# Cross-attention on one core: loads in slices and in order of use, two sets of transposes moved to the front, the mask arithmetic on another engine, the last group's normalisation in two parts

## The chip, the cores and the metric

The kernel runs on one core of one Trainium2 chip. The metric is device time in microseconds (us) of one execution; lower is better. The core has five engines that run side by side: TensorE (PE in the profile; PEld is its weight load), VectorE (DVE), ScalarE (ACT), GpSimd (POOL) and SyncE (SP). Each takes its own instructions strictly in order and waits for others by semaphores. Loads and stores are issued here from SP and ACT, each through a queue of its own, and are carried out by 16 DMA engines that both queues share.

## The reference

Cross-attention with 8 heads of width 256, 16 batches, 256 queries and 77 keys in each batch, all in float32, then a residual and a layer normalisation:

```python
Q = (img_embed @ Wq).reshape(B, -1, H, D).transpose(0, 2, 1, 3)     # img_embed = x (16, 256, 256)
K = (sent_embed @ Wk).reshape(B, -1, H, D).transpose(0, 2, 1, 3)    # sent_embed = context (16, 77, 192)
V = (sent_embed @ Wv).reshape(B, -1, H, D).transpose(0, 2, 1, 3)
score = jnp.einsum('bhqd,bhkd->bhqk', Q, K) / math.sqrt(D)
score = jnp.where((atten_mask != 0)[:, None, None, :], score, -jnp.inf)
attn = jax.nn.softmax(score, axis=-1)
ctx = jnp.einsum('bhqk,bhkd->bqhd', attn, V).reshape(B, -1, H * D)
out = ctx @ Wo + img_embed
mu = jnp.mean(out, axis=-1, keepdims=True)
var = jnp.var(out, axis=-1, keepdims=True)
return (out - mu) * jax.lax.rsqrt(var + EPS) * gamma + beta
```

## The kernel before

Neither Q, K nor V is formed. Per head two products of weights are made once: G = Wq Wk^T / sqrt(D), kept transposed in `gT`, and U = Wv Wo, in `u`. Then, per batch, A = G c^T (`a`, four batches at a time) and VW = c U (`vw`), and for each tile of 128 queries the scores x A (`ps`), a softmax over 77 keys for each of 8 heads (`s`, `e`, `p`), the transposes of `p` (`pp`, copied to `pT`), the sum over heads of p VW (`po`), the residual and the statistics for the normalisation (`mv`).

The program has three stages.

1. **Once.** All loads are issued at the head of the program: on SP's queue Wq in two halves, Wv, the first group of x (`xg`, 8 tiles of 128 rows, 1 MB), the mask `m_i`, gamma, beta and the second group of x; on ACT's queue Wk in two halves, the context `c_sb` and Wo. For each head TensorE then transposes the rows of Wq and Wk (`p_wqT`, `p_wkT`, by `transposed`) and multiplies them (`pg`); then it transposes the context in 22 pieces (`pc`, copied to `cT`), and for each head transposes Wv (`p_wvT`) and multiplies by Wo (`pu`). Transposes land in PSUM; `evacuate` copies them to SBUF, in turn by ACT and DVE. So the copies of `p_wqT` fall to ACT and those of `p_wkT` to DVE. Five small DVE operations turn the mask into `bias` and `live`.
2. **The batches.** Four groups of four batches, 8 query tiles each. `prepare_group` transposes the group's x (`px`, copied to `xT`) and makes `a` (64 matmuls `pa`); then tiles follow, with the attention of a tile two tiles behind its scores.
3. **The end of a group.** When the last tile of a group is done, one square root and one reciprocal over its 8 tiles, then 8 operations that scale and shift (line 313), and a store for each two tiles.

The order on each engine is that of the program as a scheduler rearranges it: it may move an independent instruction ahead of others on its engine, and once built the order is fixed. Buffers are pooled: the weights and the mask live in the pool `wload`, whose memory is given back after stage 1 and is taken over by `a` and other tiles of stage 2, so the first copy into `a` waits for the last readers of that pool. Loads and stores share eight completion semaphores in rotation: the ninth is issued when the first has landed, and so on.

Of the kernel before, what the change touches and what calls it, by code (L numbers as in the profile page):

```python
# [27 lines left out]
# so neither Q, K, V nor the context of a head is ever formed.  # L28
@with_exitstack
def kernel(  # L30
# [25 lines left out]

# [38 lines left out]

# [1 line left out]
    with tc.tile_pool(name="wload", bufs=1) as wp, tc.tile_pool(name="wt", bufs=2) as wt:  # L97
# [8 lines left out]
        wv_r = wv.rearrange("(t p) f -> p t f", p=LP)  # L106
        half = H * D // 2
        for i in range(2):
            cols = slice(i * half, (i + 1) * half)
            nc.sync.dma_start(wq_sb[:, :, cols], wq_r[:, :, cols])  # L110
            nc.scalar.dma_start(wk_sb[:, :, cols], wk_r[:, :, cols])
        nc.scalar.dma_start(c_sb, c_rows)
        nc.sync.dma_start(wv_sb, wv_r)
        nc.scalar.dma_start(wo_sb, wo.rearrange("(t p) f -> p t f", p=P))
        load_x(0)
        nc.sync.dma_start(m_i, mask.rearrange("b k -> (b k)").partition_broadcast(P))
        nc.sync.dma_start(gam, gamma.partition_broadcast(P))
        nc.sync.dma_start(bet, beta.partition_broadcast(P))
        load_x(1)

        def transposed(w_sb, rows, h, tag):
# [12 lines left out]
            return t_sb  # L134

        for h in range(H):
            wqT = transposed(wq_sb, P, h, "wqT")
            wkT = transposed(wk_sb, LP, h, "wkT")
            pg = ps_mm.tile([P, 2, DI], F32, tag="mm", name=f"pg_{h}")
            for lc in range(2):  # L140
                for dc in range(2):
                    nc.tensor.matmul(  # L142
                        pg[:LP, lc, :],
                        wkT[:, dc, lc * LP : (lc + 1) * LP],
                        wqT[:, dc, :],
                        start=(dc == 0),
                        stop=(dc == 1),
                    )
            nc.scalar.mul(gT[:, :, h, :], pg[:LP], D ** -0.5)

        for r in range(0, NCR, 2):
# [9 lines left out]
            for lc in range(2):  # L161
# [3 lines left out]
                )  # L165

        for h in range(H):
            wvT = transposed(wv_sb, LP, h, "wvT")
            pu = ps_mm.tile([P, 2, DI], F32, tag="mm", name=f"pu_{h}")
            for lc in range(2):  # L170
                for dc in range(2):
                    nc.tensor.matmul(  # L172
                        pu[:LP, lc, :],
                        wvT[:, dc, lc * LP : (lc + 1) * LP],
                        wo_sb[:, 2 * h + dc, :],
                        start=(dc == 0),
                        stop=(dc == 1),
                    )
# [13 lines left out]
    ap = ctx.enter_context(tc.tile_pool(name="ap", bufs=2))  # L192
    sp = ctx.enter_context(tc.tile_pool(name="sp", bufs=3))
    st = ctx.enter_context(tc.tile_pool(name="st", bufs=4))

    xT_of, a_of, vw_of, p_of, mv_of = {}, {}, {}, {}, {}

    def prepare_group(g):
        xg = xg_of[g]
        xT = xp.tile([P, 2, GT * P], F32, tag="xT", name=f"xT_{g}")  # L200
        for j in range(0, GT, 2):
            pt = ps_tr.tile([P, 4, P], F32, tag="tr", name=f"px_{g}_{j}")
            for dc in range(2):
                for i in range(2):
                    nc.tensor.transpose(  # L205
                        pt[:, 2 * dc + i, :], xg[:, j + i, dc * P : (dc + 1) * P], ident
                    )
            evacuate(
                xT[:, :, j * P : (j + 2) * P],
                pt.rearrange("p (dc i) m -> p dc (i m)", dc=2),  # L210
            )
        xT_of[g] = xT
        a = ap.tile([P, 2, GB, H, S2], F32, tag="a", name=f"a_{g}")
# [87 lines left out]

    def normalise_group(g):
        mv, yg = mv_of[g], xg_of[g]
        std = st.tile([P, GT], F32, tag="std", name=f"std_{g}", bufs=2)
        nc.scalar.activation(std, mv[:, :, 1], AF.Sqrt, bias=eps)
        rstd = st.tile([P, GT], F32, tag="rstd", name=f"rstd_{g}", bufs=2)
        nc.vector.reciprocal(rstd, std)
        for j in range(GT):
            y = yg[:, j, :]
# [13 lines left out]
    for t in range(NT + AHEAD):  # L323
# [44 lines left out]
```

## Time and profile before

| | us |
|---|---|
| median of 3 runs (lowest, highest) | 482.4 (482.24, 482.61) |
| the profiled execution, first to last instruction (span) | 480.1 |
| TensorE busy in the span | 439.0 (91%) |
| VectorE busy | 210.7 (44%) |
| ScalarE busy | 136.8 (28%) |
| GpSimd busy | 39.6 (8%) |

The profile covers one execution, from its first instruction to its last; of this execution no other time is on record than its span. The median of the runs is 2.3 us above the span. A busy share is an average over the three stages; a view by stretches shows each for itself.

### The profile page before, as it was taken

What the parts mean: (1) busy time and instruction counts of PE and PEld (TensorE: products, weight loads), DVE (VectorE), ACT (ScalarE), POOL (GpSimd) and SP (SyncE); (2) the same over time, 40 slices, a digit from 0 to 9 for tenths busy, and PEclk for the clock granted to TensorE, in tenths of its full rate; (3) what the DMA queues carried; (4) which work ended last, traced back from release to release, by engine and by line L of the source; (5) the groups of instructions that cost most, each with busy time, mean ns of one, the idle gap of its engine ahead of it and who ended that gap; (6) DMA issues with size and microseconds to landing.
All of it is one profiled execution on the core that took longest, in us unless ns stands there. A gap on an engine that the chain in (4) does not pass through costs nothing.

```text
span 480.1 us, 4689 instructions
## 1 busy us (share of the span) xinstructions
PE 439.0 (91%) x1846; PEld 298.3 (62%) x1846; DVE 210.7 (44%) x424; ACT 136.8 (28%) x242; POOL 39.6 (8%) x38
## 2 busy tenths in 40 slices
PE   1409899999999999999999999999999999999993
PEld 1307677755765875758567766585767756658572
DVE  0031223235736433375373433844735238555364
ACT  1103422223132222251333213523132134331321
POOL 0000000012112000121111101112111011121110
PEclk9859999999999999999999999999999999999997
DMA  8993000000000000022000000130000000200002
GB/s 237 256 341 106 0 1 1 0 2 0 0 1 0 1 0 0 1 87 89 0 0 1 0 0 2 53 123 0 1 1 0 1 0 1 89 0 0 2 1 87
DMA packets 13446, 17.86 MB, mean 37 GB/s; under 512 B 480, under 2 KB 12208, under 8 KB 13232
## 3 DMA queue, kind: packets, MB, share of 16 engines
q1 hardware_dynamic: 9696, 12.95, 8.9%
q10 hardware_dynamic: 3728, 4.62, 3.3%
q8 instruction: 14, 0.23, 0.2%
q14 instruction: 8, 0.07, 0.0%
HBM read 13.37 MB, written 4.19 MB: 37 GB/s over the span
## 4 chain that ended last, share of the span: by engine, by line
PE 87%; DMA 6%; DVE 3%; ACT 2%; issue 0%; DVEq 0%; ACTq 0%
PE po L293 24%; PE pv L234 22%; PE pa L218 14%; PE ps L250 14%; PE pp L289 5%; DMA m_i<-in_mask_BxS_if_dram 5%; PE pg L142 3%; PE pu L172 3%; DMA wk_sb<-in_L_xattn_Wk_dram 2%; PE px L205 2%; DVE wkT L94 1%; ACT pT L290 1%; DVE xg L313 1%; PE p_wkT L126 0%; PE p_wvT L126 0%
## 5 line engine op out<-in xcount | busy, mean ns | idle before, releaser
L293 PE MATMUL po<-vw,pT 77*128 77x256 f32 x512 | 117.2, 382 | 1.7 <-ACT pT L290 1.7
L234 PE MATMUL pv<-u,cT 96*77 96x512 f32 x256 | 113.1, 593 | 0.1
L293 PEld LDWEIGHTS po<-vw,pT 77*128 77x128 f32 x512 | 94.6, 190 | 21.3 <-ACT pT L290 9.7
L234 PEld LDWEIGHTS pv<-u,cT 96*77 96x77 f32 x256 | 37.5, 148 | 67.0 <-issue 57.8
L250 PE MATMUL ps<-a,xT 128*128 128x308 f32 x256 | 75.8, 422 | 0.0
L277 POOL TENSOR_TENSOR p<-e,rden 128x616 f32<-128x616 f32 x32 | 38.9, 1216 | 423.1 <-DVE rden L275 236.5
L218 PE MATMUL pa<-cT,gT 96*128 96x308 f32 x256 | 67.7, 422 | 0.0
L241 ACT COPY vw<-pv 77x512 f32<-77x512 f32 x64 | 37.1, 581 | 97.8 <-PE pv L234 97.5
L297 DVE TENSOR_TENSOR xg<-po,xg 128x256 f32<-128x256 f32 x32 | 13.6, 424 | 108.8 <-PE po L293 108.7
L290 ACT COPY pT<-pp 77x512 f32<-77x512 f32 x64 | 34.1, 583 | 86.5 <-PE pp L289 86.5
L218 PEld LDWEIGHTS pa<-cT,gT 96*128 96x128 f32 x256 | 48.0, 190 | 16.6
L250 PEld LDWEIGHTS ps<-a,xT 128*128 128x128 f32 x256 | 46.5, 190 | 12.4 <-issue 0.5
L289 PEld LDWEIGHTS pp<-ident,p 128*77 128x77 f32 x256 | 30.4, 148 | 11.3 <-issue 5.3
L94 DVE COPY a<-pa 128x308 f32<-128x308 f32 x32 | 15.3, 479 | 48.1 <-PE pa L218 48.1
L272 DVE TENSOR_REDUCE den<-e 128x8 f32<-128x616 f32 x32 | 25.4, 794 | 23.5 <-ACT e L270 23.4
L142 PE MATMUL pg<-wqT,wkT 128*96 128x256 f32 x64 | 18.9, 447 | 18.2 <-DVE wkT L94 18.2
L289 PE MATMUL pp<-ident,p 128*77 128x128 f32 x256 | 33.2, 272 | 0.0
L258 DVE TENSOR_TENSOR s<-ps,bias 128x616 f32<-128x616 f32 x32 | 25.6, 799 | 10.7 <-PE ps L250 10.7
L270 ACT ACTIVATE e<-s 128x616 f32<-128x616 f32 x32 | 22.9, 717 | 23.5 <-DVE s L266 23.4
L92 ACT COPY a<-pa 128x308 f32<-128x308 f32 x32 | 13.4, 418 | 48.3 <-PE pa L218 48.3
L142 PEld LDWEIGHTS pg<-wqT,wkT 128*96 128x96 f32 x64 | 11.6, 192 | 23.5 <-DVE wkT L94 19.8
L266 DVE TENSOR_TENSOR s<-s,top 128x616 f32<-128x616 f32 x32 | 25.6, 800 | 1.0
(45 smaller groups left out, 212.8 us busy)
## 6 DMA issues: line engine op xcount, KB each, us to landing
xg<-in_x_dram SPq DMA_DIRECT2D x4, 1024.0 KB, 12.5
out_dram<-xg SPq DMA_DIRECT2D x16, 256.0 KB, 2.2
wq_sb<-in_L_xattn_Wq_dram SPq DMA_DIRECT2D x2, 1024.0 KB, 12.3
wo_sb<-in_L_xattn_Wo_dram ACTq DMA_DIRECT2D x1, 2048.0 KB, 39.0
wk_sb<-in_L_xattn_Wk_dram ACTq DMA_DIRECT2D x2, 768.0 KB, 11.3
wv_sb<-in_L_xattn_Wv_dram SPq DMA_DIRECT2D x1, 1536.0 KB, 22.1
c_sb<-in_ctx_dram ACTq DMA_DIRECT2D x1, 924.0 KB, 27.3
m_i<-in_mask_BxS_if_dram SPq DMA_DIRECT2D x1, 616.0 KB, 21.7
```

What stands on the lines that cost most here:

```text
L142: nc.tensor.matmul(pg[:LP, lc, :], wkT[:, dc, lc * LP : (lc + 1) * LP], wqT[:, dc, :], start=(dc == 0), stop=(dc == 1),)
L218: nc.tensor.matmul(pa.rearrange("p b k -> p (b k)"), gT[:, lc, h, dc * P : (dc + 1) * P], cT[:, lc, g * GB * S2 : (g + 1) * GB * S2], star ...
L234: nc.tensor.matmul(pv[:S2], cT[:, lc, b * S2 : (b + 1) * S2], u[:, lc, 2 * n : 2 * n + 2, :].rearrange("p h d -> p (h d)"), start=(lc == 0 ...
L241: nc.scalar.copy(vw[:, 2 * n : 2 * n + 2, :].rearrange("p h d -> p (h d)"), pv[:S2])
L250: nc.tensor.matmul(ps[:, hh, :HK], xT_of[g][:, dc, j * P : (j + 1) * P], a_of[g][:, dc, bl, hh * 4 : hh * 4 + 4, :].rearrange("p h k -> p ...
L258: nc.vector.tensor_tensor(s.rearrange("p (a h) k -> p a h k", a=2), ps[:, :, :HK].rearrange("p a (h k) -> p a h k", k=S2), bias[:, b, :].u ...
L266: nc.vector.tensor_tensor(s, s, top.unsqueeze(2).to_broadcast([P, H, S2]), ALU.subtract)
L272: nc.vector.tensor_reduce(den, e, AX.X, ALU.add)
L277: nc.gpsimd.tensor_tensor(p, e, rden.unsqueeze(2).to_broadcast([P, H, S2]), ALU.mult)
L289: nc.tensor.transpose(pt[:S2, i, :], p[:, hh * 4 + i, :], ident)
L290: nc.scalar.copy(pT[:, hh * 4 : hh * 4 + 4, :], pt[:S2])
L293: nc.tensor.matmul(po, pT[:, h, :], vw_of[b][:, h, :], start=(h == 0), stop=(h == H - 1))
```

## The change

Four things are changed.

- **Loads.** The context goes first, its two parts on both queues; all else is issued by SP in order of use: the first group of x, then Wq and Wk in four slices of two heads each, Wv and Wo in two halves each, the second group of x, the mask, gamma, beta. The number of loads rises from 12 to 19. ACT issues one.
- **Transposes.** The transposes of the context and of the first group of x are ahead of the weight products on TensorE, and their copies ahead of the weights' copies on ACT and DVE.
- **Mask.** `bias` and `live` are computed by 14 GpSimd instructions (a compare, nine multiplications that fold 77 columns to one, four small or final ones); DVE has none of them.
- **Last group.** For the last of the four groups, the first six tiles are normalised and stored after the sixth; the last two after the eighth. The other groups are as before.

```diff
+        mid = NCR // 2
+        nc.scalar.dma_start(c_sb[:, :mid, :], c_rows[:, :mid, :])
+        nc.sync.dma_start(c_sb[:, mid:, :], c_rows[:, mid:, :])
+        load_x(0)
+        for h in range(0, H, 2):
+            cols = slice(h * D, (h + 2) * D)
             nc.sync.dma_start(wq_sb[:, :, cols], wq_r[:, :, cols])
-            nc.scalar.dma_start(wk_sb[:, :, cols], wk_r[:, :, cols])
-        nc.scalar.dma_start(c_sb, c_rows)
-        nc.sync.dma_start(wv_sb, wv_r)
-        nc.scalar.dma_start(wo_sb, wo.rearrange("(t p) f -> p t f", p=P))
-        load_x(0)
+            nc.sync.dma_start(wk_sb[:, :, cols], wk_r[:, :, cols])
+        for h in range(0, H, 4):
+            cols = slice(h * D, (h + 4) * D)
+            nc.sync.dma_start(wv_sb[:, :, cols], wv_r[:, :, cols])
+            nc.sync.dma_start(wo_sb[:, 2 * h : 2 * h + 8, :], wo_r[:, 2 * h : 2 * h + 8, :])
+        load_x(1)
         nc.sync.dma_start(m_i, mask.rearrange("b k -> (b k)").partition_broadcast(P))
         nc.sync.dma_start(gam, gamma.partition_broadcast(P))
         nc.sync.dma_start(bet, beta.partition_broadcast(P))
-        load_x(1)
...
+        transpose_x(0)
+
         for h in range(H):
             wqT = transposed(wq_sb, P, h, "wqT")
...
-        bias_f = bias.rearrange("p b k -> p (b k)")
-        nc.vector.tensor_scalar(bias_f, m_i, 0.0, None, ALU.not_equal)
-        some = wp.tile([P, B], F32, tag="some", name="some")
-        nc.vector.tensor_reduce(some, bias, AX.X, ALU.max)
-        nc.vector.reciprocal(live, some)
-        nc.vector.tensor_tensor(live, live, some, ALU.mult)
-        nc.vector.tensor_scalar(bias_f, bias_f, 1.0, MASKED, ALU.subtract, ALU.mult)
+        nc.gpsimd.tensor_scalar(bias_f, m_i, 0.0, None, ALU.is_equal)
+        none = wp.tile([P, B, S2 // 2], F32, tag="none", name="none")
+        left, n = bias, S2
+        while n > 1:
+            n, odd = n // 2, n % 2
+            nc.gpsimd.tensor_tensor(none[:, :, :n], left[:, :, :n], left[:, :, n : 2 * n], ALU.mult)
+            if odd:
+                nc.gpsimd.tensor_tensor(
+                    none[:, :, :1], none[:, :, :1], left[:, :, 2 * n : 2 * n + 1], ALU.mult
+                )
+            left = none
+        none = none[:, :, 0]
+        nc.gpsimd.tensor_scalar(none, none, MASKED, MASKED, ALU.mult, ALU.mult)
+        nc.gpsimd.tensor_tensor(live, none, none, ALU.subtract)
+        nc.gpsimd.tensor_scalar(live, live, 1.0, None, ALU.add)
+        nc.gpsimd.tensor_scalar(bias_f, bias_f, -MASKED, None, ALU.mult)
...
-    def normalise_group(g):
+    def normalise(g, first, last):
...
+            if d // GT == NG - 1:
+                if d % GT == GT - QT - 1:
+                    normalise(d // GT, 0, GT - QT)
+                elif d % GT == GT - 1:
+                    normalise(d // GT, GT - QT, GT)
+            elif d % GT == GT - 1:
+                normalise(d // GT, 0, GT)
```

What the built programs hold, at three places. First VectorE at its head, before the change; `wkT` are the copies of the transposed Wk of heads 0, 1 and 2, and the rows between them make `bias` and `live`:

```order
L66 MEMSET eps 128x1
L94 COPY wkT_117<-p_wkT_118 128x384
L184 TENSOR_SCALAR bias<-m_i 128x1232
L186 TENSOR_REDUCE some<-bias 128x16
L187 RECIPROCAL live<-some 128x16
L189 TENSOR_SCALAR bias<-bias 128x1232
L94 COPY wkT_137<-p_wkT_138 128x384
L188 TENSOR_TENSOR live<-live,some 128x16
L94 COPY wkT_157<-p_wkT_158 128x384
```

The same place with the change:

```order
L95 COPY cT<-pc_145 96x224
L95 COPY cT<-pc_152 96x112
L95 COPY xT_157<-px_2_164 128x2x256
L95 COPY xT_157<-px_6_176 128x2x256
L95 COPY wkT_189<-p_wkT_190 128x384
L95 COPY wkT_209<-p_wkT_210 128x384
L95 COPY wkT_229<-p_wkT_230 128x384
```

The scheduler had put four of the mask's operations behind the copy of head 0 and ahead of that of head 1; they are gone from this engine, and the copies of the context and of x stand ahead of the weights' copies.

Second, TensorE at its head, before the change (`p_wqT` and `p_wkT` are transposes of weights, `pg` the product of a head):

```order
L126 MATMUL p_wqT_111<-ident,wq_sb 128x128 x4
L126 MATMUL p_wkT_118<-ident,wk_sb 128x96 x4
L126 MATMUL p_wqT_131<-ident,wq_sb 128x128 x4
L142 MATMUL pg_124<-wqT_110,wkT_117 96x256 x4
L126 MATMUL p_wkT_138<-ident,wk_sb 128x96 x4
L126 MATMUL p_wqT_151<-ident,wq_sb 128x128 x4
L142 MATMUL pg_144<-wqT_130,wkT_137 96x256 x4
```

With the change, from the fifth of the six tiles `pc` of the context on:

```order
L164 MATMUL pc_145<-ident,c_sb 96x112 x4
L164 MATMUL pc_152<-ident,c_sb 96x112 x2
L106 MATMUL px_0_158<-ident,xg_98 128x128 x4
L106 MATMUL px_2_164<-ident,xg_98 128x128 x4
L106 MATMUL px_4_170<-ident,xg_98 128x128 x4
L106 MATMUL px_6_176<-ident,xg_98 128x128 x4
L149 MATMUL p_wqT_183<-ident,wq_sb 128x128 x4
L149 MATMUL p_wkT_190<-ident,wk_sb 128x96 x4
L149 MATMUL p_wqT_203<-ident,wq_sb 128x128 x4
L183 MATMUL pg_196<-wqT_182,wkT_189 96x256 x4
L149 MATMUL p_wkT_210<-ident,wk_sb 128x96 x4
L149 MATMUL p_wqT_223<-ident,wq_sb 128x128 x4
```

All 22 transposes of the context and all 16 of x came from behind the products to the head; within the heads' part nothing changed places. From the first `pa` of the first group on, the order on TensorE is the same in both programs.

Third, VectorE at the end of the program, before the change (`po` the attention of the last two tiles, `bn` and `mv` their statistics):

```order
L297 TENSOR_TENSOR xg_1665<-po_2544,xg_1665 128x256
L299 BN_STATS bn_2554<-xg_1665 128x6
L300 BN_AGGR mv_2078<-bn_2554 128x2
L310 SCALAR_TENSOR_TENSOR xg_1665<-xg_1665,mv_2078,gam 128x256
L297 TENSOR_TENSOR xg_1665<-po_2570,xg_1665 128x256
L299 BN_STATS bn_2580<-xg_1665 128x6
L300 BN_AGGR mv_2078<-bn_2580 128x2
L310 SCALAR_TENSOR_TENSOR xg_1665<-xg_1665,mv_2078,gam 128x256
L307 RECIPROCAL rstd_2585<-std_2583 128x8
L313 SCALAR_TENSOR_TENSOR xg_1665<-xg_1665,rstd_2585,bet 128x256 x8
```

And with it:

```order
L329 RECIPROCAL rstd_0_2549<-std_0_2547 128x6
L335 SCALAR_TENSOR_TENSOR xg_1681<-xg_1681,rstd_0_2549,bet 128x256 x6
L319 TENSOR_TENSOR xg_1681<-po_2579,xg_1681 128x256
L321 BN_STATS bn_2589<-xg_1681 128x6
L322 BN_AGGR mv_2094<-bn_2589 128x2
L332 SCALAR_TENSOR_TENSOR xg_1681<-xg_1681,mv_2094,gam 128x256
L319 TENSOR_TENSOR xg_1681<-po_2605,xg_1681 128x256
L321 BN_STATS bn_2615<-xg_1681 128x6
L322 BN_AGGR mv_2094<-bn_2615 128x2
L332 SCALAR_TENSOR_TENSOR xg_1681<-xg_1681,mv_2094,gam 128x256
L329 RECIPROCAL rstd_6_2620<-std_6_2618 128x2
L335 SCALAR_TENSOR_TENSOR xg_1681<-xg_1681,rstd_6_2620,bet 128x256 x2
```

Six of the eight operations of the old line 313 now stand ahead of the last two tiles' additions, two behind them.

## Rows read from the trace of the kernel before

**Rows 1.** Page, part 1: busy us of each engine, share of the span, instructions.
```profile
PE 439.0 (91%) x1846; PEld 298.3 (62%) x1846; DVE 210.7 (44%) x424; ACT 136.8 (28%) x242; POOL 39.6 (8%) x38
```

**Rows 2.** Busy time by stretch: start and end, length, engines, PEclk, DMA share, GB/s.
```profile
0.00:80.00 80.00, 48.89 (x261) 36.78 (x262) 15.95 (x29) 16.64 (x32) 0.70 (x6) 0.89 0.50 141
80.00:472.00 392.00, 390.07 (x1587) 261.50 (x1586) 189.89 (x383) 119.83 (x209) 38.93 (x32) 1.00 0.04 14
```

**Rows 3.** Timeline, first 43 us: start, us, engine, line, operation [idle before, releaser].
```profile
10.24 1.09 PE L126 MATMUL p_wqT<-ident,wq_sb 128*128 128x128 f32 x4 [10.24 <-DMA wq_sb<-in_L_xattn_Wq_dram]
...
17.58 0.69 PE L126 MATMUL p_wqT<-ident,wq_sb 128*128 128x128 f32 x4
...
31.40 0.80 DVE L184 TENSOR_SCALAR bias<-m_i 128x1232 f32<-128x1232 int32 x1 [18.84 <-DMA m_i<-in_mask_BxS_if_dram]
...
35.13 3.48 PE L142 MATMUL pg<-wqT,wkT 128*96 128x256 f32 x8 [16.86 <-DVE wkT L94]
...
38.78 0.60 PE L126 MATMUL p_wqT<-ident,wq_sb 128*128 128x128 f32 x4
...
39.60 1.97 PE L142 MATMUL pg<-wqT,wkT 128*96 128x256 f32 x8 [0.21 <-DVE wkT L94]
...
42.55 1.97 PE L142 MATMUL pg<-wqT,wkT 128*96 128x256 f32 x8 [0.21 <-DVE wkT L94]
```

**Rows 4.** Busy time by stretch of 5 us, columns as in rows 2.
```profile
0.00:5.00 5.00, 0.00 (x0) 0.00 (x0) 0.06 (x1) 1.28 (x1) 0.70 (x6) 1.00 0.64 172
5.00:10.00 5.00, 0.00 (x0) 0.00 (x0) 0.00 (x0) 0.00 (x0) 0.00 (x0) 1.00 1.03 280
10.00:15.00 5.00, 4.10 (x16) 3.42 (x17) 0.56 (x1) 1.17 (x2) 0.00 (x0) 1.00 1.05 302
15.00:20.00 5.00, 3.27 (x14) 2.26 (x12) 0.00 (x0) 1.18 (x2) 0.00 (x0) 1.00 1.04 238
...
25.00:30.00 5.00, 0.00 (x0) 0.00 (x0) 0.00 (x0) 0.00 (x0) 0.00 (x0) 0.50 1.10 344
```

**Rows 5.** Page, part 6: DMA issues, count, KB each, median us to landing.
```profile
out_dram<-xg SPq DMA_DIRECT2D x16, 256.0 KB, 2.2
...
c_sb<-in_ctx_dram ACTq DMA_DIRECT2D x1, 924.0 KB, 27.3
m_i<-in_mask_BxS_if_dram SPq DMA_DIRECT2D x1, 616.0 KB, 21.7
```

**Rows 6.** Line 84, loads of x: landing; and a stretch within the last one.
```profile
DMA to landing us min/median/max: 5.2/12.5/27.1
...
316.80:317.30 0.50, 0.50 (x4) 0.44 (x3) 0.00 (x0) 0.00 (x0) 0.00 (x0) 1.00 1.08 383
```

**Rows 7.** Timeline, 56 to 97 us, TensorE, columns as in rows 3.
```profile
57.65 0.97 PE L156 MATMUL pc<-ident,c_sb 112*96 112x112 f32 x8 [0.57 <-DVE cT L94]
...
59.48 1.20 PE L126 MATMUL p_wvT<-ident,wv_sb 96*128 96x96 f32 x8
...
65.24 3.69 PE L172 MATMUL pu<-wo_sb,wvT 128*96 128x256 f32 x16 [0.29 <-ACT wvT L92]
...
69.89 3.69 PE L172 MATMUL pu<-wo_sb,wvT 128*96 128x256 f32 x16 [0.29 <-ACT wvT L92]
...
78.07 1.04 PE L205 MATMUL px<-ident,xg 128*128 128x128 f32 x8
...
80.39 16.23 PE L218 MATMUL pa<-cT,gT 96*128 96x308 f32 x62
```

**Rows 8.** Groups by shape, GpSimd: line, operation, shapes, count | busy us, mean ns.
```profile
L277 POOL TENSOR_TENSOR p<-e,rden 128x616 f32<-128x616 f32 x32 | 38.9, 1216 | 423.1 <-DVE rden L275 236.5 <-PE po L293 163.7 <-PE pv L234 22.2
```

**Rows 9.** Timeline, last 12 us, columns as in rows 3.
```profile
468.19 3.72 PE L293 MATMUL po<-vw,pT 77*128 77x256 f32 x16 [0.29 <-ACT pT L290]
...
473.73 3.26 DVE L313 SCALAR_TENSOR_TENSOR xg<-xg,rstd,bet 128x256 f32<-128x256 f32 x8
474.64 2.75 SPq L318 DMA_DIRECT2D out_dram<-xg  x4
```

More of the change, by code (lines that the diff above doesn't have):

```diff
@@ L71 @@
     bias = const.tile([P, B, S2], F32, tag="bias", name="bias")
+    bias_f = bias.rearrange("p b k -> p (b k)")
     live = const.tile([P, B], F32, tag="live", name="live")
@@ L94, in evacuate, with transpose_x @@
             nc.vector.tensor_copy(dst, src)
+    xT_of = {}
+    def transpose_x(g):
+        xg = xg_of[g]
+        xT = xp.tile([P, 2, GT * P], F32, tag="xT", name=f"xT_{g}")
+        for j in range(0, GT, 2):
+            pt = ps_tr.tile([P, 4, P], F32, tag="tr", name=f"px_{g}_{j}")
+            for dc in range(2):
+                for i in range(2):
+                    nc.tensor.transpose(
+                        pt[:, 2 * dc + i, :], xg[:, j + i, dc * P : (dc + 1) * P], ident
+                    )
+            evacuate(
+                xT[:, :, j * P : (j + 2) * P],
+                pt.rearrange("p (dc i) m -> p dc (i m)", dc=2),
+            )
+        xT_of[g] = xT
     with tc.tile_pool(name="wload", bufs=1) as wp, tc.tile_pool(name="wt", bufs=2) as wt:
@@ L106 @@
         wv_r = wv.rearrange("(t p) f -> p t f", p=LP)
-        half = H * D // 2
-        for i in range(2):
-            cols = slice(i * half, (i + 1) * half)
-            nc.sync.dma_start(wq_sb[:, :, cols], wq_r[:, :, cols])
-            nc.scalar.dma_start(wk_sb[:, :, cols], wk_r[:, :, cols])
-        nc.scalar.dma_start(c_sb, c_rows)
-        nc.sync.dma_start(wv_sb, wv_r)
-        nc.scalar.dma_start(wo_sb, wo.rearrange("(t p) f -> p t f", p=P))
-        load_x(0)
+        wo_r = wo.rearrange("(t p) f -> p t f", p=P)
+        mid = NCR // 2
[4 more added lines that the diff above has]
+            cols = slice(h * D, (h + 2) * D)
+            nc.sync.dma_start(wq_sb[:, :, cols], wq_r[:, :, cols])
+            nc.sync.dma_start(wk_sb[:, :, cols], wk_r[:, :, cols])
[4 more added lines that the diff above has]
+        load_x(1)
         nc.sync.dma_start(m_i, mask.rearrange("b k -> (b k)").partition_broadcast(P))
@@ L134, in transposed @@
             return t_sb
[L136 to L149, printed above, removed]
         for r in range(0, NCR, 2):
@@ L165 @@
                 )
+        transpose_x(0)
+        for h in range(H):
+            wqT = transposed(wq_sb, P, h, "wqT")
+            wkT = transposed(wk_sb, LP, h, "wkT")
+            pg = ps_mm.tile([P, 2, DI], F32, tag="mm", name=f"pg_{h}")
+            for lc in range(2):
+                for dc in range(2):
+                    nc.tensor.matmul(
+                        pg[:LP, lc, :],
+                        wkT[:, dc, lc * LP : (lc + 1) * LP],
+                        wqT[:, dc, :],
+                        start=(dc == 0),
+                        stop=(dc == 1),
+                    )
+            nc.scalar.mul(gT[:, :, h, :], pg[:LP], D ** -0.5)
         for h in range(H):
@@ L179 @@
             evacuate(u[:, :, h, :], pu[:LP])
-        bias_f = bias.rearrange("p b k -> p (b k)")
-        nc.vector.tensor_scalar(bias_f, m_i, 0.0, None, ALU.not_equal)
-        some = wp.tile([P, B], F32, tag="some", name="some")
-        nc.vector.tensor_reduce(some, bias, AX.X, ALU.max)
-        nc.vector.reciprocal(live, some)
-        nc.vector.tensor_tensor(live, live, some, ALU.mult)
-        nc.vector.tensor_scalar(bias_f, bias_f, 1.0, MASKED, ALU.subtract, ALU.mult)
+        nc.gpsimd.tensor_scalar(bias_f, m_i, 0.0, None, ALU.is_equal)
[7 more added lines that the diff above has]
+                    none[:, :, :1], none[:, :, :1], left[:, :, 2 * n : 2 * n + 1], ALU.mult
+                )
+            left = none
[4 more added lines that the diff above has]
+        nc.gpsimd.tensor_scalar(bias_f, bias_f, -MASKED, None, ALU.mult)
     ap = ctx.enter_context(tc.tile_pool(name="ap", bufs=2))
@@ L194 @@
     st = ctx.enter_context(tc.tile_pool(name="st", bufs=4))
-    xT_of, a_of, vw_of, p_of, mv_of = {}, {}, {}, {}, {}
+    a_of, vw_of, p_of, mv_of = {}, {}, {}, {}
     def prepare_group(g):
[L199 to L212, printed above, removed]
+        if g:
+            transpose_x(g)
         a = ap.tile([P, 2, GB, H, S2], F32, tag="a", name=f"a_{g}")
@@ L300, in attend @@
         nc.vector.bn_aggr(mv_of[g][:, j, :], bn)
-    def normalise_group(g):
+    def normalise(g, first, last):
         mv, yg = mv_of[g], xg_of[g]
[L304 to L308, printed above, removed]
+        std = st.tile([P, GT], F32, tag="std", name=f"std_{g}_{first}", bufs=2)
+        nc.scalar.activation(std[:, first:last], mv[:, first:last, 1], AF.Sqrt, bias=eps)
+        rstd = st.tile([P, GT], F32, tag="rstd", name=f"rstd_{g}_{first}", bufs=2)
+        nc.vector.reciprocal(rstd[:, first:last], std[:, first:last])
+        for j in range(first, last):
             y = yg[:, j, :]
@@ L332 @@
             attend(d)
-            if d % GT == GT - 1:
-                normalise_group(d // GT)
+            if d // GT == NG - 1:
[5 more added lines that the diff above has]
+                normalise(d // GT, 0, GT)
                 if d // GT + 2 < NG:
```

## The prediction

> **What bounds the kernel now.** I read the page's totals first: TensorE is busy 91% of the span, all others under half [rows 1]. A share over the whole span hides stages, so I split it next. Between 80 and 472 us TensorE is busy 390.1 of 392.0 us [rows 2]: this part is TensorE's work and nothing else, and no edit takes a TensorE instruction out of it. What can be won lies in the first 80 us, where TensorE is busy for 48.9 [rows 2], and behind its last matmul.
>
> The timeline shows where the first 80 us go. TensorE starts at 10.24, when Wq's first half has landed, and idles once more, for 16.86 us, until the second product at 35.13; the wait is for the DVE copy of head 1's Wk [rows 3]. DVE is not busy then: it stands for 18.84 us in front of the mask's compare until the mask lands, and only after the mask work does the copy come. So a wait that reads "TensorE on DVE" is a wait on a 0.63 MB load [rows 5] that nobody needs before the first scores. Meanwhile the loads run without pause: 0.86 MB by 5 us, 2.26 by 10, 3.77 by 15 [rows 4]. The clock shows too: at 25 to 30 us, TensorE idle, it is granted 0.50 of 2.4 GHz, and the eight `pg` matmuls behind the gap take 3.48 us against 1.97 later; in the first 10 us the page has 1.00, yet the four transposes at 10.24 take 1.09 us against 0.60 at 38.78 [rows 3, 4]. So TensorE's first work is slow as well.
>
> **The change, part by part.** The measure is when the 64 `pa` begin, since all behind them stays as it is. The 62 `pa` from 80.39 take 16.23 us, 0.26 each [rows 7]; with the two ahead of them the stage begins in effect at 79.9.
>
> *Context.* It is now first, on both queues: 0.95 MB (924 KB [rows 5]), which at the pace of rows 4 is moved by 5.3 us. How long after that does a transfer count as landed? The first halves of Wq and Wk, 1.83 MB, were moved by 8.5 at the earliest, and TensorE went on at 10.24 [rows 3, 4], so 0 to 1.7; I take 1. The context lands at 6.3; at 238 GB/s, the stretch in which its short rows were part of the mix [rows 4], a microsecond later. Its 22 transposes: eight took 0.97 at full clock, and the ten from 57.65 to 59.48 took 0.18 each with their waits for copies [rows 7]; slow by 1.09/0.60 they take 0.22. So 4.0 to 4.8; most of it will be slow, I take 4.6: done at 10.9.
>
> *x.* With it 2.00 MB are moved by 9.1, landed by 10.1, so the context's transposes cover it. Its 16 transposes took 78.07 to 80.39, 2.3 us, at full clock [rows 7], and would take 16 x 0.27 = 4.4 at half. After the second idle stretch the clock was back between 35.13 and 38.78, 3.6 us; the first time, with gaps between, only by 17.58 [rows 3]. I take 2.9: done at 13.8.
>
> *First slice of Wq and Wk.* 2.91 MB moved by 12.2, landed at 13.2, just covered. Three times four transposes of about 0.6 and a wait for the copy, 1.9: the first `pg` at 15.7. In slow clock throughout and with the context late, it would be 18 to 20; fast from the middle of the context on, 14.
>
> *The heads' products.* The mask work no longer stands in front of head 1, so seven steps of 2.95 (39.60 to 42.55) and a last 1.97 follow each other [rows 3]: 38.3. A slice feeds two heads, 5.9 us, and its 0.92 MB take 3.1 us at 300 GB/s, so later slices stay ahead; the second lands near 16.2, wanted at 18.2. U took from 59.48 to 78.07, 18.6 us, in steps of 4.65 for two heads [rows 7]; its halves end at 7.5 and 9.3 MB of the stream, at 0.28 MB a us near 28 and 34, wanted at 38 and 47. The order moves its first transposes ahead of the last `pg`; I take 18.5: done at 56.8. The `pa` follow with a wait of 0.4 for the copy of the last `pu`: **57.2 instead of 79.9, 22.7 us**. The transposes of context and x cost nothing behind the products any more; they are paid ahead of the first slice, where TensorE would wait for the loads.
>
> *More loads on one queue.* Does SP's queue alone carry the pace? The last x load did, alone: 383 GB/s in its middle, and 5.2 us from issue to landing for 1.05 MB [rows 6]. SP waits for the landing of the load eight places earlier before it issues one; with seven others in the queue at some 0.5 MB each, that costs no gap. The Trainium skill (DMA: Bandwidth & Descriptors, Rules for kernel authors) asks for 1 MiB or more a load, and its fit gives each load 2.0 us beside its bytes; slices of 0.4 to 0.5 MB go against that. Were these 2.0 us paid one after the other, the estimate is a sum of 460. Above, the fixed part of a load overlaps with its neighbours'; the four stores at the end show such overlap, all issued within 2.75 us at 2.2 us each [rows 5, 9].
>
> *Mask on GpSimd.* Two operations over 1232 elements, one over 608, one over 304 and ten of 144 or fewer. The only elementwise row of GpSimd is `p`, 616 elements in 1216 ns [rows 8], 1.97 ns an element. By it the four large ones take 6.8 and the ten small, 0.1 to 0.3 each, 1 to 2.5: 8 to 9 us. Compare and integer input are not in the trace; I bound them by the 0.80 of the same compare on DVE [rows 3] (4 us in all) and three times `p`'s pace (25 us). I take 8.5, being nearest to the row. The mask ends at 11.0 MB of the stream, at 0.28 to 0.30 MB a us near 38 to 41. The chain ends at about 49, and the first copy into `a`, which takes over the pool's memory, is due at 57.7. So it costs nothing; the cover is 8 to 9 us. x's second group and gamma, beta are due far later.
>
> *The end.* After the last `po` (468.19 + 3.72), DVE scales eight tiles in 3.26 us, and SP issues four stores from 474.64 on over 2.75 us, the last when the last tiles are done [rows 9]. Now six tiles and three stores are ahead of that; the last store takes the place of the first, at 474.64 instead of 477.0: **2.4 us**. The six operations, some 2.5 us, fall into the time in which DVE waits for tile 30's `po`; they may hold its addition by 1 us, while tile 31's comes 4.9 us later. The square root's table load moves between two copies of `pT` where ACT idles.
>
> *Sum.* 22.7 + 2.4 = 25.1 us from the profiled execution's 480.1 gives a span of 455.0; the median of the runs lies 2.3 above the old span, and I carry that over: **457.3 us**.
>
> **The rivals.**
> 1. *The clock stays low* through context, x and first head: 6.3 + 4.8 + 4.4 + 3.4 puts the first `pg` near 19, and it takes 1.5 more. Near 462. For it: after 10.24, with gaps, four transposes at 17.58 were the first at 0.69 us [rows 3]. Against: here the two sets leave TensorE hardly a gap. 0.15.
> 2. *Loads set the pace*, by short rows, one queue or fixed costs one after the other. At 238 GB/s throughout, the first slice lands near 15.8, the second near 20, and two late slices cost 2 to 4 us: 460. The page's rule, read as serial, ends at the same time. Against: 383 GB/s from SP alone [rows 6]. 0.13.
> 3. *The mask's chain holds `a`.* Both copying engines stop at their first copy into `a`, TensorE two `pa` later. At 20 to 30 us the chain ends at 60 to 70 and costs 2 to 12 us: 460 to 470. The Trainium skill (GPSIMD Engine Reference, Engine selection) says that elementwise work belongs on VectorE, GpSimd being about 2x slower with two inputs. That alone, against DVE's 3 us of mask work, stays inside the cover. 0.06.
> 4. *Slower than before*, by the same mechanism: the chain would have to end past 57.7 + 25.1 = 82.8, that is last 42 us or more, 5 times `p`'s pace over all 14. 0.03.
> 5. *The change doesn't do what it says*: the stream of loads, 11.3 MB, is as long as before, and if all products had to wait for its end nothing would come at the start but the mask's 17 us less what is lost by context and x being ahead. The programs' order speaks against it, each head waiting for its own slice. 0.01 for a time within 0.2% of before.
>
> **How the numbers follow.** The forecast as worked out, first `pg` between 14 and 17.5, has 0.62: 455.5 to 459.2. Below it no case is left but a context that lands and a clock that rises at their earliest. Adding rivals 1 and 2, 0.90 is reached at 454.8 to 462.5; that is my range. A measurement here tells 0.2%, 1 us. Faster: all but rival 4 and the last, 0.96; same 0.01; slower 0.03.
>
> **What would show it.** Right: no DVE wait for the mask; TensorE's first work near 6 to 7 us on the context, the first `pg` at 14 to 17.5, no wait above 2 us between it and `pa`; `pa` from 57 on; some 398 us from there to the end (400.2 before, less 2.4); a last store some 3 us after the last scale. Wrong: the first copy of `a` released by GpSimd; `p_wqT` of heads 2, 4 or 6 released by a load; a TensorE stage past `pa` longer than before.

## The result, and the profile after

The changed kernel takes **458.43 us** (median of 4 executions, 458.19 to 459.18), the kernel before 482.32 (482.1 to 482.61) on the same chip: ratio 0.9494, 95% interval 0.9471 to 0.9516. The prediction was 457.3 us, range 454.8 to 462.5.

The profiled execution has a span of 457.4 us; it is the slowest of the four, the other spans are 456.4 to 456.7. Time less span is 1.8 us in each of them, and in an execution of the kernel before (481.75 with a span of 480.0).

The busy times of the engines in the whole span, which answer to [rows 1]:

```profile
PE 439.1 (96%) x1846; PEld 298.3 (65%) x1846; DVE 207.6 (45%) x420; ACT 137.0 (30%) x243; POOL 51.0 (11%) x52
```

TensorE does the same 439 us of work in a span that is 22.7 us shorter: idle time went. GpSimd has 14 instructions more.

Busy times by stretch, columns as in [rows 2]; the first two rows cover the program up to 450 us, the other three answer to [rows 4]:

```profile
0.00:60.00 60.00, 49.27 (x264) 37.20 (x265) 12.96 (x25) 17.38 (x33) 12.14 (x20) 1.00 0.64 189
60.00:450.00 390.00, 388.26 (x1578) 260.11 (x1577) 192.17 (x389) 119.33 (x209) 38.88 (x32) 1.00 0.05 16
0.00:5.00 5.00, 0.00 (x0) 0.00 (x0) 0.06 (x1) 1.28 (x1) 0.69 (x6) 1.00 0.59 162
5.00:10.00 5.00, 2.91 (x15) 2.43 (x16) 0.78 (x2) 0.88 (x3) 0.00 (x0) 1.00 1.10 339
10.00:15.00 5.00, 4.41 (x21) 3.27 (x19) 1.88 (x5) 1.66 (x5) 0.00 (x0) 1.00 1.07 296
```

From 60 us on TensorE is as full as before. All that is left to win at the head is in the first 60 us, where it is busy for 49.

TensorE's timeline at the head and where the batches begin (columns as in [rows 3]):

```profile
6.98 5.00 PE L164 MATMUL pc<-ident,c_sb 112*96 112x112 f32 x22 [6.98 <-DMA c_sb<-in_ctx_dram]
12.46 3.87 PE L106 MATMUL px<-ident,xg 128*128 128x128 f32 x16 [0.48 <-DVE cT L95]
16.12 1.06 PE L149 MATMUL p_wqT<-ident,wq_sb 128*128 128x128 f32 x4
17.11 0.90 PE L149 MATMUL p_wkT<-ident,wk_sb 96*128 96x96 f32 x4
17.86 0.78 PE L149 MATMUL p_wqT<-ident,wq_sb 128*128 128x128 f32 x4
18.66 1.97 PE L183 MATMUL pg<-wqT,wkT 128*96 128x256 f32 x8
...
39.32 1.97 PE L183 MATMUL pg<-wqT,wkT 128*96 128x256 f32 x8 [0.32 <-DVE wkT L95]
...
57.86 1.97 PE L197 MATMUL pu<-wo_sb,wvT 128*96 128x256 f32 x8 [0.62 <-ACT wvT L93]
59.67 0.68 PE L240 MATMUL pa<-cT,gT 96*128 96x308 f32 x2
```

The wait of 16.86 us is gone: none is longer than 0.7 us between the first transpose and `pa`, and none is released by a load. `pa` begins at 59.67 (79.9 in effect before). But TensorE's work up to 17.8 us is slow: four transposes of Wq take 1.06 us where [rows 3] have 0.60 later. The column of the granted clock prints 1.00 (2.4 GHz) in these first stretches, as it did before the change. The durations say the lower level, 1.2 GHz, and I go by them: x's 16 transposes take 3.87 us here, and 3.86 us in e6 below, where the column prints 0.50.

### The profile page after: what moved, and what is told of

It is laid out like the page before. It is cut to its first block, busy times and chain, and to the rows that moved or that the text cites. A ratio compares the mean times of both kernels' runs of the same rounds, so it can differ in the third digit from the quotient of the medians.

```text
span 457.4 us, 4720 instructions
## 1 busy us (share of the span) xinstructions
PE 439.1 (96%) x1846; PEld 298.3 (65%) x1846; DVE 207.6 (45%) x420; ACT 137.0 (30%) x243; POOL 51.0 (11%) x52
## 3 DMA queue, kind: packets, MB, share of 16 engines
q1 hardware_dynamic: 14048, 17.14, 12.4%
## 4 chain that ended last, share of the span: by engine, by line
PE 94%; DVE 2%; ACT 1%; DMA 1%; issue 0%; DVEq 0%; ACTq 0%
PE po L315 25%; PE pv L256 24%; PE ps L272 15%; PE pa L240 15%; PE pp L311 6%; PE pg L183 3%; PE pu L197 3%; PE px L106 2%; DMA c_sb<-in_ctx_dram 1%; DVE wkT L95 1%; ACT pT L312 1%; PE p_wkT L149 1%; PE pc L164 1%; ACT wvT L93 0%; PE p_wqT L149 0%
## 5 line engine op out<-in xcount | busy, mean ns | idle before, releaser
L319 DVE TENSOR_TENSOR xg<-po,xg 128x256 f32<-128x256 f32 x32 | 13.6, 424 | 104.7 <-PE po L315 104.7
L272 PEld LDWEIGHTS ps<-a,xT 128*128 128x128 f32 x256 | 46.5, 190 | 12.4 <-issue 0.5
L311 PEld LDWEIGHTS pp<-ident,p 128*77 128x77 f32 x256 | 30.4, 148 | 11.3 <-issue 5.3
L287 DVE TENSOR_REDUCE top<-s 128x8 f32<-128x616 f32 x32 | 25.4, 795 | 1.1
L183 PE MATMUL pg<-wqT,wkT 128*96 128x256 f32 x64 | 15.7, 389 | 1.6 <-DVE wkT L95 1.6
## 6 DMA issues: line engine op xcount, KB each, us to landing
wv_sb<-in_L_xattn_Wv_dram SPq DMA_DIRECT2D x2, 768.0 KB, 15.7
```

The source lines that it names most:

```text
L183: nc.tensor.matmul(pg[:LP, lc, :], wkT[:, dc, lc * LP : (lc + 1) * LP], wqT[:, dc, :], start=(dc == 0), stop=(dc == 1),)
L272: nc.tensor.matmul(ps[:, hh, :HK], xT_of[g][:, dc, j * P : (j + 1) * P], a_of[g][:, dc, bl, hh * 4 : hh * 4 + 4, :].rearrange("p h k -> p ...
L287: nc.vector.tensor_reduce(top, s, AX.X, ALU.max)
L311: nc.tensor.transpose(pt[:S2, i, :], p[:, hh * 4 + i, :], ident)
```

## The experiments

Each is a change of one kernel; the ratio is always to the kernel before, run on the same chip.

**e1_mask_alone.** The kernel before with only the mask on GpSimd (the 14 instructions of the diff above), loads, transposes and end as before.

> The kernel before with one part of the change: the mask arithmetic on GpSimd, all else as it was. Theory (the wait of the second product on the mask was the bulk of the loss): the second product starts near 18.5 instead of 35.1 us and at full clock, the heads' products end near 38.2, the transposes of the context near 41.3, so all behind comes 18 us earlier: 464 us. Rival (the loads set the start whatever TensorE does, since their stream is 41 us long): Wo lands at 41 and U waits for it, so at most 12 us are won: 470 us or more.

Measured: 462.9 us, ratio 0.9585 (0.9559 to 0.9611). On TensorE:

```profile
13.53 3.62 PE L142 MATMUL pg<-wqT,wkT 128*96 128x256 f32 x8
...
18.16 1.97 PE L142 MATMUL pg<-wqT,wkT 128*96 128x256 f32 x8 [0.21 <-DVE wkT L94]
```

The second product stands at 18.16 instead of 35.13. Freeing VectorE from the wait for the mask is by itself worth 482.45 - 462.9 = 19.55 of the 23.9 us.

**e2_mask_back.** The changed kernel with the five mask operations on VectorE again.

```diff
-        nc.gpsimd.tensor_scalar(bias_f, m_i, 0.0, None, ALU.is_equal)
...
+        nc.vector.tensor_scalar(bias_f, m_i, 0.0, None, ALU.not_equal)
+        nc.vector.tensor_reduce(some, bias, AX.X, ALU.max)
...
```

> The changed kernel with the mask arithmetic back on VectorE; loads, transposes and the two-part end stay. The scheduler now puts the five operations behind the last copy of Wk, where the mask (landed at 39.6 us) is just there. Theory (what counts is that no copy TensorE needs stands behind the mask's wait, not which engine computes it): 458.5 to 460 us, the copy of the first U late by at most 1 us. Rival (taking the mask off VectorE is needed for the gain, as in the prediction's first term): the time goes up by several us, 465 us or more.

Measured: 458.68 us, ratio 0.9498 (0.9468 to 0.9528): the same as the changed kernel. VectorE's timeline shows why:

```profile
37.95 0.56 DVE L95 COPY wkT<-p_wkT 128x384 f32<-128x384 f32 x1 [2.39 <-PE p_wkT L149]
39.79 0.80 DVE L208 TENSOR_SCALAR bias<-m_i 128x1232 f32<-128x1232 int32 x1 [1.28 <-DMA m_i<-in_mask_BxS_if_dram]
...
43.01 0.68 DVE L95 COPY u<-pu 96x512 f32<-96x512 f32 x1
```

With the loads and transposes in the new order, the scheduler puts the compare behind the last copy of `wkT`, where the mask has nearly landed. So the wait has two cures, either of which is enough: another engine (e1), or another place in VectorE's order (e2).

**e3_end_whole.** The changed kernel with the last group normalised in one piece, as before.

> The changed kernel with the last group normalised in one piece, as before. Theory: the end is 2.4 us longer and nothing else moves: 460.8 us. Rival (the six early operations on VectorE and the earlier table load had cost as much as they saved): 458.4 us, no difference.

Measured: 461.16 us, ratio 0.9549 (0.9522 to 0.9575), 2.7 us more. The two-part end is worth 2.7, and 462.9 - 461.16 = 1.7 is left for loads and transposes once the mask is out of the way (e1 and e3 ran on the same chip, and their executions do not overlap).

**e4_warm_matmuls, e5_warm_short.** The changed kernel with useless matmuls on a tile of zeros ahead of the context's transposes: 14, then 7. Their result is not used.

```diff
+        hot = wp.tile([P, DI], F32, tag="hot", name="hot")
+        nc.vector.memset(hot, 0.0)
+        pw = ps_sc.tile([P, 2, 512], F32, tag="sc", name="pw")
+        for i in range(7):
+            nc.tensor.matmul(pw[:, 0, :DI], ident, hot, start=True, stop=True)
```

> The changed kernel with 14 matmuls of no use (128 by 128 identity against 128 by 256 zeros, into a PSUM tile that stage 2 overwrites) at the head of TensorE, before the context has landed. Theory (the slow clock from 7.0 to 17.8 us is a matter of what TensorE did before; work ahead of the context raises the clock earlier): the 22 transposes of the context take 0.12 to 0.18 us each instead of 0.24, those of x 0.15, the first product starts 3 to 4.5 us earlier, near 14.5 us: 454 to 455.5 us. Rival (the clock rises at a fixed time after the program's start, as it did near 17.5 us in both profiles): 458.4 us. Third possibility: the transposes don't hold the clock up, and it falls back: 456 to 458.5 us.

Measured: 459.21 us, ratio 0.9504 (0.9478 to 0.9531), no gain. Fourteen were too many: they last to 10.0 us, the transposes of the context begin at 9.84 instead of 6.98, though eight take 0.93 us then, and the first product comes at 18.64.

> The changed kernel with 7 useless matmuls at its head instead of 14 (the 14 ended at 10.0 us, 3 us after the context had landed, and gave back what the faster clock won). Theory (the slow clock of the context's and x's transposes is what the sum was short of): they end near 7.0 us, the transposes run at full clock, the first product starts near 15.7 instead of 18.7 us: 455.5 us. Rival (the faster transposes run into the loads of x or of the first slice, or into the copies): 457 to 458.5 us.

Measured: **455.96 us**, ratio 0.9443 (0.9418 to 0.9468). TensorE's timeline of e5 (the trace has two passes for each of the 7 matmuls):

```profile
1.34 5.40 PE L163 MATMUL pw<-hot,ident 128*128 128x256 f32 x14 [1.34 <-POOL ident masks.py:199]
6.57 0.93 PE L170 MATMUL pc<-ident,c_sb 112*96 112x112 f32 x8
...
10.85 1.09 PE L106 MATMUL px<-ident,xg 128*128 128x128 f32 x8 [0.66 <-DVE cT L95]
...
13.52 0.66 PE L149 MATMUL p_wqT<-ident,wq_sb 128*128 128x128 f32 x4
...
15.37 1.97 PE L189 MATMUL pg<-wqT,wkT 128*96 128x256 f32 x8
```

They run while the context is still on its way, so they delay next to nothing. The context is done at 10.85 and the first product comes at 15.37, 3.3 us earlier than in the changed kernel; what that one lost against e5 was the clock. That 10.85 and 15.37 are near the 10.9 and 15.7 of the prediction is in part chance, since the prediction had counted most of the context at the low clock.

**e6_warm_transposes.** The same with 20 useless transposes.

> As the run with 7 useless matmuls, but with 20 useless transposes of the identity (about the same time at the slow clock). If transposes raise the clock as matmuls do: 455.5 us, and the context's transposes at 0.12 us each. If they don't, which would explain why the clock stayed low for 10.8 us of transposes in the changed kernel: context still at 0.24 us each, 458.4 us.

Measured: 457.48 us, ratio 0.9473 (0.9438 to 0.9507), spread widely (455.95 to 458.73).

```profile
1.34 4.27 PE L161 MATMUL pw<-ident 128*128 128x128 f32 x20 [1.34 <-POOL ident masks.py:199]
6.88 0.97 PE L168 MATMUL pc<-ident,c_sb 112*96 112x112 f32 x8 [1.27 <-DMA c_sb<-in_ctx_dram]
8.32 2.94 PE L168 MATMUL pc<-ident,c_sb 112*96 112x112 f32 x14 [0.47 <-DVE cT L95]
11.74 3.86 PE L106 MATMUL px<-ident,xg 128*128 128x128 f32 x16 [0.48 <-DVE cT L95]
```

A stretch of its busy times, columns as in [rows 2]:

```profile
12.00:14.00 2.00, 2.00 (x10) 1.78 (x10) 0.26 (x1) 0.59 (x1) 0.00 (x0) 0.50 1.05 341
```

Transposes do raise the clock: the first eight of the context take 0.97 us, as fast as in [rows 7]. But they end early, TensorE waits 1.27 us for the context, and from 8.32 on the next 14 take 0.21 us each and x's 16 take 3.86 us: it fell back. Here the column of the granted clock shows it, 0.50 from 10 to 14 us.

**e7_mask_chain_long.** The changed kernel with the mask's compare done seven times, to test the price of a late chain (rival 3).

> The changed kernel with the mask's compare done seven times instead of once; at 3.33 us each the GpSimd chain ends near 72 instead of 52.0 us. Theory (the first copy into a waits for the last reader of the weights' pool): that copy, at 61.0 us in the changed kernel, comes near 72, TensorE stops two pa after its start: 458.4 + 11 = 469.5 us. Rival (the wait isn't real, only the scores near 77 us need the mask): 458.4 us, no difference.

Measured: 472.46 us, ratio 0.978 (0.9751 to 0.9809). GpSimd, ScalarE and TensorE, a row or two of each timeline:

```profile
39.26 23.75 POOL L209 TENSOR_SCALAR bias<-m_i 128x1232 f32<-128x1232 int32 x7 [37.97 <-DMA m_i<-in_mask_BxS_if_dram]
...
71.53 0.21 POOL L222 TENSOR_TENSOR live<-none 128x16 f32<-128x16 f32 x1
...
71.78 0.42 ACT L93 COPY a<-pa 128x308 f32<-128x308 f32 x1 [14.96 <-POOL live L222]
...
72.25 17.40 PE L241 MATMUL pa<-cT,gT 96*128 96x308 f32 x56 [11.33 <-ACT a L93]
```

The first copies into `a` wait for GpSimd's last reader of the old pool, TensorE stops for 11.33 us, and the granted clock of 65 to 75 us is 0.50. The 56 `pa` behind the gap take 17.40 us instead of 56/64 of 16.6 = 14.5. Gap and slow restart, 11.3 + 2.9 = 14.2, are the 14.0 us measured.

**e8_weights_first.** The changed kernel with the slices of Wq and Wk loaded first, and context and x with their transposes behind.

> The changed kernel with the slices of Wq and Wk loaded first, context and first x behind them, and the transposes of context and x back behind the products, as before. Theory (context and x ahead of the products only reorder TensorE's work, since TensorE has no gap to hide them in; what counts is when its first work lands and how soon the clock rises, and products raised it in 4 us, the transposes only after 10.8): first product near 9.8, all behind 4 us earlier than with the mask alone, with the two-part end: 456 us. Rival (the transposes were hidden in the wait for the first slice, as the prediction said): 460 us or more.

Measured: 462.08 us, ratio 0.9561 (0.9526 to 0.9595). This does not tell the theories apart: the built order differs in the products too. The transposes of Wq are split 3 + 1 around the products, each head waits 0.3 to 0.7 us for ScalarE's copy, and a step takes 3.3 us (14.39 to 34.37 for six) instead of 2.95. The clock fell as well: the granted clock is 0.50 from 42 to 44 us, behind the context's transposes with their short waits, and the first 16 `pu` take 5.32 us where the next take 3.69.

```profile
41.60 5.32 PE L193 MATMUL pu<-wo_sb,wvT 128*96 128x256 f32 x16 [0.24 <-ACT wvT L93]
```

e10 asks a narrower question in its place.

**e9_warm_onecopy.** e5 with each tile of the context's transposes copied to SBUF by one copy instead of two.

> The changed kernel with seven useless matmuls ahead of the context's transposes, as in the run before of that kind (455.96 us), and with each tile of the context's transposes copied to SBUF by one copy instead of two. Theory, the copies set the pace of the context's transposes once the clock is up: they start at 6.6 and are done near 9.7 instead of 10.85, the first product comes near 14.6, the time is 455.2. Rival, the loads hold what follows: x is landed near 9.7 to 10 and the first slice near 12.9, so the time stays at 456.

Measured: 456.47 us, ratio 0.9447 (0.9418 to 0.9476): no gain over e5. From its first transpose (7.34) to the first of x (11.41) it takes 4.1 us, in e5 4.3. The theory fell: fewer copies are worth 0.2 us here. The times of the two runs don't measure this, since in the profile of e9 the useless matmuls themselves took 6.17 us, 0.8 more than in e5.

**e10_x_behind.** The changed kernel with x's first group back behind the slices, and its transposes behind the products.

```diff
-        load_x(0)
         for h in range(0, H, 2):
...
+        load_x(0)
...
-        transpose_x(0)
...
-        if g:
-            transpose_x(g)
+        transpose_x(g)
```

> The changed kernel with the first group of x loaded behind the slices of Wq and Wk and its transposes behind the products, as before the change; the context stays first. Theory of the prediction, the transposes of x were hidden in the wait for the first slice: they come back on the path behind the products at full clock, 2.3 us, and the time is 460.7. Rival, at the low clock the first slice had landed before TensorE was through, so the transposes ahead (3.9 us) were on the path as they would be behind (2.3): the time is 458.4 or up to 1.6 us less.

Measured: 457.93 us, ratio 0.9484 (0.9448 to 0.9519), not to be told from the changed kernel. TensorE at its head:

```profile
6.47 4.99 PE L164 MATMUL pc<-ident,c_sb 112*96 112x112 f32 x22 [6.47 <-DMA c_sb<-in_ctx_dram]
11.95 1.12 PE L149 MATMUL p_wqT<-ident,wq_sb 128*128 128x128 f32 x4 [0.48 <-DVE cT L95]
...
14.65 2.29 PE L181 MATMUL pg<-wqT,wkT 128*96 128x256 f32 x8
```

TensorE goes straight from the context to Wq with no wait for the slice. Moving x's load and transposes to the front hid nothing: it only moved them.

**e11_two_queues.** The changed kernel with the slices of Wk issued by ACT's queue.

```diff
-            nc.sync.dma_start(wk_sb[:, :, cols], wk_r[:, :, cols])
+            nc.scalar.dma_start(wk_sb[:, :, cols], wk_r[:, :, cols])
```

> The changed kernel with the four slices of Wk issued by ACT's queue instead of SP's. Theory, the loads stay ahead of TensorE and one queue carries the pace: 458.4, no difference. Rival, SP's one queue (issues of 5 to 7 us) delays the first slice: the first product comes 1 to 2 us earlier, 456 to 457.

Measured: 462.16 us, ratio 0.9568 (0.9539 to 0.9598), 3.7 us slower than the changed kernel; neither theory had this.

```profile
6.99 4.99 PE L164 MATMUL pc<-ident,c_sb 112*96 112x112 f32 x22 [6.99 <-DMA c_sb<-in_ctx_dram]
15.77 3.70 PE L106 MATMUL px<-ident,xg 128*128 128x128 f32 x16 [3.78 <-DMA xg<-in_x_dram]
```

The first x takes 14.5 us from issue to landing, in the changed kernel 8.4. The sum of all bytes does not explain it: by 15 us 3.7 MB are moved (164, 287 and 293 GB/s in stretches of 5 us), in the changed kernel 4.0. But the four slices of Wk, which are not needed yet, now move at the same time as x: the first of them landed at 9.5 us, x at 15.6. The Trainium skill (DMA: Bandwidth & Descriptors, Rules for kernel authors) says that spreading loads over issuing engines brings no bandwidth, since all run on the same 16 engines and interleave. By that rule the trace agrees, and adds the price of the interleaving.

**e12_warm_x_behind.** e5 and e10 together.

> The two edits that the runs before point to, together: seven useless matmuls ahead of the context's transposes, and the first group of x loaded behind the slices of Wq and Wk with its transposes behind the products. Theory: the context's transposes end at 10.85 as with the matmuls alone, the first slice has landed by then (near 10.5), and the first product comes at 12.8 instead of 15.4; of these 2.6 us the 16 transposes behind the products take 1.5 to 2.3 back, so the time is 455.0, between 454.8 and 455.9. Rival, the first slice lands later than 11.5 and TensorE waits: 456.5.

Measured: **455.32 us** (454.49 to 456.87), ratio 0.9447 (0.9412 to 0.9482); spans 452.7 to 453.6, those of e5 454.0 to 454.2.

```profile
9.47 0.78 PE L170 MATMUL pc<-ident,c_sb 112*96 112x112 f32 x6 [0.47 <-DVE cT L95]
10.91 0.66 PE L149 MATMUL p_wqT<-ident,wq_sb 128*128 128x128 f32 x4 [0.66 <-DVE cT L95]
...
12.74 1.89 PE L187 MATMUL pg<-wqT,wkT 128*96 128x256 f32 x8
```

The first product is at 12.74, as the theory had it, and x's transposes behind the products take a part of it back. By the times it can't be told from e5; the spans say about 1 us less, and in two of its four executions the part of the time outside the span was 3.2 us instead of 1.8. Every execution of both is faster than every one of the changed kernel.

## Why the prediction was right, and where it was off

- **What bounded the kernel.** Right. TensorE from `pa` on was left as it was, and the won time is the idle time at the head. The wait that read "TensorE on DVE" was a wait on the mask's load: e1 removes that alone and wins 19.5 us. From the first `pa` to the end of the span it is 397.7 us, some 398 predicted.
- **Landing of the context.** Predicted 6.3, TensorE went on at 6.98; inside the bounds, 0.7 late.
- **Context, x and first head: the mis-sized term.** The prediction took the clock to be up in the middle of x's transposes. It was up only near 17.8 (in the profile of e2, with the same work ahead of the products, by 15.87, and the first `pg` came at 17.92). The context took 5.5 us with its waits instead of 4.6, x 3.7 instead of 2.9, the first head 2.5 instead of 1.9. With the late landing, the first `pg` came 3.0 us late, at 18.66 instead of 15.7, and outside the forecast's 14 to 17.5. e5 shows the cause: with work for TensorE before the context lands, it is at 15.37. The clock is not all of it: with the clock up throughout, as in e5, the prediction's own terms give 6.3 + 4.0 + 2.3 + 1.9 = 14.5, and the other 0.9 us are the start at 6.57 and the waits for copies between the transposes (context 4.3, x 2.7). Rival 1 came about by two thirds: first `pg` near 19, but at full speed (1.97 us), so that it cost 3.0 us and not 4.7.
- **Transposes "paid ahead of the first slice, where TensorE would wait for the loads".** This fell for x (e10); for the context alone no run tried it. By the prediction's own numbers loads and transposes were to bring 22.7 less the wait of 16.86 and the slow product's 1.5, that is 4.3 us; they brought 1.7. With the clock up, e5 has 462.9 - 455.96 - 2.7 = 4.2, but e1 was not run with useless matmuls, and its first product is slow too (3.62 us), so how much of the 4.2 belongs to loads and transposes is not shown.
- **Heads and U.** Right to 0.1: from the first `pg` to the end of the last 22.6 us, U 18.5 more. The wait of 0.4 ahead of `pa` did not come. So `pa` began at 59.67, not 57.2.
- **Loads.** Right that SP's queue carries the pace: no `p_wqT` waits for a load, x landed at 9.6 (10.1 predicted) and the first slice at 12.8 (13.2). e11 adds that a second queue would have hurt. Rival 2's first slice near 15.8 is too late by its own rate: 0.86 MB by 5 us and the other 2.05 MB at 238 GB/s are moved by 13.6 and landed at 14.6. The Trainium skill (DMA: Bandwidth & Descriptors, Anatomy of one DMA — SWDGE (gpsimd) path) gives each load about 2.0 us beside its bytes, by a fit to loads that GpSimd issues, where SP issues these; read as paid one after the other, the trace does not agree, since the DMA engines stay full (a share of 1.05 and more from 5 to 35 us) and rival 2's waits do not come.
- **Mask on GpSimd.** Free, as predicted, though its chain was longer. GpSimd's timeline, first and last rows and the four large operations:

```profile
39.58 3.33 POOL L208 TENSOR_SCALAR bias<-m_i 128x1232 f32<-128x1232 int32 x1 [38.29 <-DMA m_i<-in_mask_BxS_if_dram]
42.99 1.27 POOL L213 TENSOR_TENSOR none<-bias 128x608 f32<-128x608 f32 x1
...
44.67 0.84 POOL L213 TENSOR_TENSOR none<-none 128x304 f32<-128x304 f32 x1
45.59 3.33 POOL L223 TENSOR_SCALAR bias<-bias 128x1232 f32<-128x1232 f32 x1
...
51.75 0.26 POOL L222 TENSOR_SCALAR live<-live 128x16 f32<-128x16 f32 x1
```

  The mask landed at 39.6 (38 to 41 predicted); the chain took 12.4 us, not 8.5, since the two one-input operations run at 2.7 ns an element instead of `p`'s 1.97, which makes 1.8 us, and the ten small ones take 3.7 with the gaps between them where 1 to 2.5 had been allowed. It ended at 52.0, the first copy into `a` came at 60.9: 8.9 us of cover were left, and e7 shows what lies beyond it. e2 shows that GpSimd was not needed for it.
- **The end.** Right: 2.4 predicted, 2.7 measured (e3). In the changed kernel's last 13 us, six operations and three stores are out of the way early (the stores are issued at 446.17, 446.96 and 447.75, the fourth at 454.24):

```profile
445.26 2.46 DVE L335 SCALAR_TENSOR_TENSOR xg<-xg,rstd,bet 128x256 f32<-128x256 f32 x6
446.17 8.45 SPq L340 DMA_DIRECT2D out_dram<-xg  x4
...
453.33 0.88 DVE L335 SCALAR_TENSOR_TENSOR xg<-xg,rstd,bet 128x256 f32<-128x256 f32 x2
```

- **The sum.** The span was 457.4, predicted 455.0: 2.4 too much, from the head (3.0 late, less 0.4 for the wait that did not come). The median missed by only 1.1, for two reasons that are no merit: the profiled execution is the slowest of the four by 0.7 to 1.0, and the part of the time outside the span is 1.8 us, not the 2.3 that I carried over from a span of one execution and a median of others.

What stays open: why the scheduler put the mask's operations behind the first copy before and behind the last in e2 (its rules were not tried), why TensorE's clock fell in e6 and e8 behind waits this short, and where it stood in the executions without a trace.

## What to carry to other kernels

On an engine that works strictly in order, look behind a wait on a copy for the instruction ahead of that copy: here it was a load that nobody needed yet, and it was enough to move either the work or its place in the order. Loads that are needed in sequence belong on one queue; in e11 a second queue moved no more bytes and made the load that was needed first land 6 us later. Work moved into the head of this program was paid at TensorE's low clock, so cost it by the durations of the first stretch, or give TensorE something useless to do while the first load is on its way and no longer.

## What was not expected of the hardware

- **The clock at the head.** In the changed kernel TensorE's durations are those of the low level for 10.8 us, from 6.98 to 17.8, through the 38 transposes of context and x, with short waits between them, and those of the first weights. Seven useless matmuls from 1.34 on had it up when they ended at 6.7 (e5). Useless transposes had it up as well, but it fell again behind a wait of 1.27 us and one of 0.47 (e6, 0.50 granted from 10 to 14 us). In e8 it fell to 0.50 behind the context's transposes, with no wait longer than 0.71 us. After the 11.33 us gap of e7 the granted clock was 0.50, and the work behind it took 2.9 us longer.
- **GpSimd with one input.** The compare of 1232 elements takes 3.33 us on GpSimd and 0.80 on VectorE [rows 3], a factor of 4.2. With two inputs `p` takes 1.22 us for 616 elements, and VectorE's subtraction of the row maximum, of the same size, 0.80: a factor of 1.5. The Trainium skill (GPSIMD Engine Reference, Engine selection) has it the other way round, about 2x slower for two inputs and "roughly line-rate" for one; here the measurement decides.
- **Issues that block.** SP was held for 5 to 7 us in three of the later load issues, with the DMA engines full up to 35 us, and TensorE waited for no load behind it, so it cost nothing:

```profile
14.37 5.19 SPq L137 DMA_DIRECT2D wv_sb<-in_L_xattn_Wv_dram  x1
...
20.20 4.87 SPq L85 DMA_DIRECT2D xg<-in_x_dram  x1
25.11 7.04 SPq L140 DMA_DIRECT2D m_i<-in_mask_BxS_if_dram  x1
```
